# Moving gathered and scattered rows of a four-layer graph network from GpSimd to the SyncE and ScalarE queues, and splitting the K and V products over the halves of the array

## The chip, the core and the metric

The kernel runs on one core of a Trainium2 chip. The core has five engines with a queue of instructions each: TensorE (PE, its weight loads shown apart as PEld), VectorE (DVE), ScalarE (ACT), GpSimd (POOL) and SyncE (SP), which only issues transfers. All transfers run on the same 16 DMA engines. The metric is the time of one execution on the device in microseconds (us).

## What is computed

A graph with 12,500 nodes of 64 features and 400,000 edges, sorted by their target `dst`, goes through four layers, each followed by a residual sum and a layer norm. Cut to what matters:

```python
# layer 0: a message for every edge, the maximum over the edges of each target
h = relu(concat([x[dst], x[src] - x[dst]]) @ W1 + b1); out = segment_max(h @ W2 + b2, dst)
# layer 1: the mean of the edge attributes over the edges of each source
v_e = segment_sum(edge_attr, src) / max(count(src), 1)
out = relu(relu(concat([x, v_e, u]) @ W1 + b1) @ W2 + b2)
# layer 2: the mean of x[src] over the edges of each target, times a count of gates, a product
h = segment_sum(x[src], dst) / max(deg, 1); ...; out = (h * gates) @ W_lin.T + b_lin
# layer 3: attention with a weight matrix for each node type (4) and edge type (8), 4 heads
k, q, v = typed_linear(x, W, node_type)
a = (rel_att(k[src]) * rel_att(q[dst])).sum(-1) * rel_pri / sqrt(16)
out = typed_linear(segment_sum(softmax_over_dst(a) * rel_msg(v[src]), dst), Wa, node_type)
```

All is in float32 to the outside; `src` is random, so every x[src] is a gather of single rows.

## The kernel before, in words

Edges lie on 128 partitions ("lanes") of 3,125 consecutive edges each. A column of 128 edges, one for each lane, is called a tile; 25 columns are a group (`G`), 125 groups in all, in the edge loops 124 and three short ones. A running result goes along each lane: `keep` is 1 where an edge has the same target as the one before, so that `previous * keep + new` adds up a segment (line 1127 in layer 2, 1278 for q in layer 3). Results of all edges are written to memory (R0 to R3), and the row of each node's last edge is gathered from there.

Every gather of 128 rows is an indirect DMA on GpSimd, issued by the helper `gather` (line 211). The stages in the order of time:

- **Early part** (to about 1,270 us): 40 groups of x[src] are gathered for later use, counts are made by one-hot products on PE.
- **Scatter** (to about 5,380 us): the edge attributes, sorted anew by `src`, are scattered into the table SRT. `advance` (DVE, PE and ACT, in an order fixed by the program) works out the places of a group's edges in rounds of four tiles, `hot` loads the attributes into the buffer `at` (four buffers; lines 632 and 634: DVE writes the number of the source beside them), and `scatter` (line 734) sends 25 tiles of a group by indirect DMAs. It runs two groups behind `advance`. SP also writes zeros into the table S here.
- **Layer 0, with the sums of layer 1** (to about 8,140 us): gathers `gb` from TB; at the end the ends of lanes are put right (`ends_of_lanes`, `put_ends`).
- **Node stage of layers 0 and 1** (`nodes01`, to about 8,415 us): for each of 98 node tiles a gather from R0 (`ga`) and one from R1 (`g1`), blocks of 7.
- **Layer 2** (to about 12,280 us): gathers `gx` from X2, four buffers of a group; ACT's queue writes the sums to R2 (line 1130). In every third group, 3 to 123, the last tile is not gathered by GpSimd: SP loads 16 row numbers into registers (line 1112) and issues 16 DMAs of one row each (line 1117), eight times over. A row's address is worked out from its number by an instruction of its own.
- **Node stage of layers 2 and 3** (`nodes2`, to about 12,600 us): blocks of 7 node tiles in stages that interleave; a gather from R2, the gates, the layer norm, the products for q, k and v by node type (line 1221 writes K and V of a block into `kv`, K in partitions 0 to 63, V in 64 to 127), a put of the q rows into S by GpSimd (line 308), and for each tile two products of `kv` with `wkm` (line 1244), which ACT copies (line 1246) to `km` and SP writes to the table TKM: for each node and edge type 64 numbers of K and 64 of V. `wkm` has 128 rows; in each of its columns one half of them is zero.
- **Layer 3** (to about 16,550 us): gathers `gk` from TKM (3 buffers), loads of S into `st` (2 buffers, line 1273), then scores, running maximum, sums and messages, written to R3 by SP (line 1324).
- **Last node stage**: gathers from R3, the output product and the last layer norm.

A queue runs in order: an instruction that waits holds all that stand behind it in the same queue. Where the kernel says `manual_schedule(engines=...)`, these engines take the order in which the program is written; elsewhere a scheduler chooses it when the kernel is built.

Of the kernel before, what the change touches and what calls it, by code (L numbers as in the profile page):

```python
# [43 lines left out]
ACTN = 3  # L44
ROWS2 = 3
RL = 16
ZC = 200
# [3 lines left out]
def resnorm_gnn_kernel(ctx: ExitStack, tc: tile.TileContext, a: dict, out: bass.AP):  # L51
# [158 lines left out]
    def gather(to, table, at):  # L210
        return nc.gpsimd.indirect_dma_start(  # L211
            out=to, out_offset=None, in_=table, in_offset=bass.IndirectOffsetOnAxis(ap=at, axis=0)
        )

    def same_keys(psp, sb, key, n, each=None, want_count=False):
# [188 lines left out]

    wkm = const.tile([P, ETY, 2, D], F32, name="wkm")
    nc.vector.memset(wkm, 0.0)
    for h in range(NH):
        nc.sync.dma_start(
            wkm[D + h * HS : D + (h + 1) * HS, :, 1, h * HS : (h + 1) * HS],
            a["L3_gnn_rel_msg"][h].rearrange("t d o -> d t o"),  # L410
        )
# [226 lines left out]
    def turned(k):  # L638
# [6 lines left out]
        for j in range(m):  # L645
            nc.tensor.matmul(pT[:, j, :], oh[:, j, :], identh, start=True, stop=True)  # L646
        pH = ups.tile([NT, 2, P], F32, name="pH")
        for s, n in ((0, min(2, m)), (1, m)):
# [57 lines left out]
    now = [begin]  # L706
    todo = [0]

    def advance():

        k = todo[0]
        hot(k + 2)
        turned(k + 1)
        ol = work[k]["hots"][1]
        pG = spots(k)
        if k + 2 in work:
            work[k + 2]["tables"] = tables(now[0])
        pairs(k + 1)
        sums_of(k, pG, ol)
        todo[0] += 1  # L720

# [8 lines left out]
    def scatter(i, between=()):  # L730
        at, _, to = placed.pop(i)
        for j in range(G):

# [7 lines left out]
            if j % 4 == 0 and between:  # L741
# [3 lines left out]
                puts0.append(row)  # L745
        return put

# [73 lines left out]
    with tc.tile_pool(name="ini", bufs=1) as ini, tc.tile_pool(name="inips", bufs=1, space=PSUM) as ips:  # L821
# [31 lines left out]
        for t in range(ETY):  # L853
            pr_ = ips.tile([P, 4, P], F32, name="ps_k")[:D, 0, :D]
            nc.tensor.transpose(pr_, ratt[:, t, :], ident[:D, :D])
            rT = ini.tile([D, D], F32, name="rT", bufs=2)
            nc.vector.tensor_copy(rT, pr_)
            pg = ips.tile([P, 4, P], F32, name="ps_k")[:D, 0, :D]
            nc.tensor.matmul(pg, rT, rT, start=True, stop=True)
            nc.vector.tensor_scalar(wkm[:D, t, 0, :], pg, prib[:, t : t + 1], None, op0=ALU.mult)  # L860

# [59 lines left out]

    to_l0.close()

    with (tc.tile_pool(name="e0", bufs=2) as sb, tc.tile_pool(name="e0ps", bufs=2, space=PSUM) as psp,
# [81 lines left out]
        for g, (c0, ng) in enumerate(groups):  # L1006
# [25 lines left out]
            while done < NG and done * R1G <= g * NG:  # L1032
                key, pm1 = sums(done, key, pm1)
                done += 1
                if done == NG:
                    end_sums()
        row = ends_of_lanes(sb, R0, D)
        ps = carry_over(ps1, sb, pm)
        u = sb.tile([D, P], F32, name="u0", bufs=1)
        nc.vector.tensor_tensor_scan(u, neg64, ps, NEG, ALU.add, ALU.max)  # L1040
        nc.vector.tensor_max(row, row, shifted(ps1, sb, u, "g0"))
        put_ends(R0, row)


    with tc.tile_pool(name="n1", bufs=1) as sb, tc.tile_pool(name="n1ps", bufs=2, space=PSUM) as psp:
# [5 lines left out]
        def nodes01(b, t0, nt):  # L1051
# [6 lines left out]
            for j in range(nt):  # L1058
                gather(ga[:, j, :], R0[: E + 1, :], lastE[:, t0 + j : t0 + j + 1])
            g1 = tile_of([P, nt, D + 1], "g1")  # L1060
            for j in range(nt):
                gather(g1[:, j, :], R1[: E + 1, :], lastE1[:, t0 + j : t0 + j + 1])
            comb = tile_of([P, nt, 2 * D], "comb", 8)
# [27 lines left out]

        in_turn(nodes01, [NB] * (NBA - 1) + [4, 2, 1], lambda n: EVERY1)


    with tc.tile_pool(name="e2", bufs=2) as sb, tc.tile_pool(name="e2ps", bufs=1, space=PSUM) as psp:
        pm = sb.tile([P, D], F32, name="m2", bufs=1)
        nc.vector.memset(pm, 0.0)

        single = [g for g in range(2, NG - 1) if g % ROWS2 == 0]
        ns = len(single)  # L1100
        assert single == list(range(single[0], NG - 1, ROWS2)) and ns <= P
        at = groups[single[0]][0] + G - 1
        sf = sb.tile([P, ns], F32, name="sf", bufs=1)
        nc.vector.tensor_copy(sf, srcS[:, at : at + (ns - 1) * ROWS2 * G + 1 : ROWS2 * G])
        ps = psp.tile([P, P], F32, name="ps_i")
        nc.tensor.transpose(ps[:ns, :], sf, ident)
        numbers = sb.tile([P, P], I32, name="numbers", bufs=1)
        nc.vector.tensor_copy(numbers[:ns, :], ps[:ns, :])

        def row_by_row(to, k):  # L1110
            for p in range(0, P, RL):
                _, rows = nc.values_load_multi_w_load_instructions(
                    numbers[k : k + 1, p : p + RL], engines=[mybir.EngineType.SP], min_val=0, max_val=NP - 1,
                    skip_runtime_bounds_check_because="src is the number of a node",
                )
                for r, row in enumerate(rows):
                    nc.sync.dma_start(to[p + r : p + r + 1, :], X2[ds(row, 1), :])

        for g, (c0, ng) in enumerate(groups):
            gx = sb.tile([P, ng, D], F32, name="gx", bufs=4)  # L1120
            if g in single:
                row_by_row(gx[:, ng - 1, :], single.index(g))
            for j in range(ng - (g in single)):
                gather(gx[:, j, :], X2, srcS[:, c0 + j : c0 + j + 1])
            for j in range(ng):
                c = c0 + j
                nc.vector.scalar_tensor_tensor(gx[:, j, :], pm, keep[:, c : c + 1], gx[:, j, :],  # L1127
                                               op0=ALU.mult, op1=ALU.add)
                pm = gx[:, j, :]
            nc.scalar.dma_start(lanes(R2)[:, c0 : c0 + ng, :], gx)  # L1130
        row = ends_of_lanes(sb, R2, D)
# [33 lines left out]
    with tc.tile_pool(name="n2", bufs=1) as sb, tc.tile_pool(name="n2ps", bufs=2, space=PSUM) as psp:  # L1165
        puts = []

        def nodes2(b, t0, nt):
# [65 lines left out]
            for j in range(nt):  # L1234
# [5 lines left out]
                s = slice(j * P, (j + 1) * P)  # L1240
                km = sb.tile([P, 2, ETY * D], F32, name=f"km_{j % 4}")
                for w in range(2):
                    pw = psp.tile([P, ETY * D], F32, name="pw", bufs=4)
                    nc.tensor.matmul(pw, kv[:, s], wkm[:, w * ETY // 2 : (w + 1) * ETY // 2].rearrange("p e s f -> p (e s f)"),  # L1244
                                     start=True, stop=True)
                    nc.scalar.activation(km[:, w, :], pw, AF.Copy)
                r = (t0 + j) * P
                nc.sync.dma_start(
                    TKM[r * ETY : (r + P) * ETY, :].rearrange("(p e) f -> p (e f)", e=ETY),
                    km.rearrange("p w f -> p (w f)"),  # L1250
                )
# [6 lines left out]
    with tc.tile_pool(name="e3", bufs=2) as sb, tc.tile_pool(name="e3ps", bufs=1, space=PSUM) as psp:  # L1258
# [8 lines left out]
        last = G  # L1267
        for c0, ng in groups:
            gk = sb.tile([P, ng, 2 * D], F32, name="gk", bufs=3)
            for j in range(ng):  # L1270
                gather(gk[:, j, :], TKM, stS[:, c0 + j : c0 + j + 1])
            st = sb.tile([P, ng, D], F32, name="st", bufs=2)
            load = nc.sync.dma_start(st, lanes(S)[:, c0 : c0 + ng, :])
            for put in puts:
                after(load, put, "reads what they write")
            for j in range(ng):
                c = c0 + j
# [46 lines left out]
            nc.sync.dma_start(lanes(R3)[:, c0 : c0 + ng, :], R)  # L1324
            last = ng

        row = ends_of_lanes(sb, R3, W3)
# [113 lines left out]
```

## Time and profile before

| what | value |
|---|---|
| median of 3 runs | 16696.17 us (16695.95 to 16697.46) |
| profiled execution, as timed | 16699.22 us |
| span of its profile | 16697.4 us |
| indirect DMAs on GpSimd: scatter, layer 3, layer 2, layer 0 | 3125, 3125, 3084, 2125 |
| single-row DMAs on SP in layer 2 | 5248 (41 tiles) |
| mean rate of all transfers | 98 GB/s, 1640.30 MB |

A row of the costliest groups has the line, the engine, the operation, what it writes and reads, the count, then the busy time in us and the mean of one in ns, then the idle time of that engine just before these instructions with what ended most of it. "issue" means that the engine waited for nothing that the profile shows. A row of the waits has who waited, for whom, the time in all, how often, and the longest. Instructions of SP and of the other engines' sequencers (marked q) are not counted as busy.

### The profile page before, as it was taken

The numbers are of one execution on the slowest core, as the hardware profiler recorded it, in microseconds if no ns is written. First come the engines' busy times: TensorE is split into PE (matmuls) and PEld (weight loads), VectorE is DVE, ScalarE is ACT, GpSimd is POOL, SyncE is SP. The second block draws the span as 40 slices with busy tenths as digits, with TensorE's granted clock in tenths as the row PEclk, the third lists the DMA queues.
The fourth block names the chain that finished last, engine by engine and source line by source line (L and its number), as shares of the span: only waits on it lengthen the run. The fifth ranks groups of instructions, "written<-read, shape, count | busy, mean of one in ns | idle before, by whom it ended". The sixth has DMA issues, their size and how long they took to land. (4 is left out here: it accounts for less than half of the span.)

```text
span 16697.4 us, 162726 instructions
## 1 busy us (share of the span) xinstructions
PE 5362.8 (32%) x42392; PEld 4426.1 (27%) x42392; DVE 9601.6 (58%) x28242; ACT 2673.4 (16%) x4960; POOL 12548.5 (75%) x13066
## 2 busy tenths in 40 slices
PE   4445666666653666666400000000051000000002
PEld 4444555554542555555300000000030000000002
DVE  9996777777753777776322222222235565555556
ACT  0012333333321111111100000000022122122112
POOL 7777777777777777777777777777776777777776
PEclk6667777777766777777655555555575555555555
DMA  2333333222222555555211111111143333333333
GB/s 81 119 103 90 85 85 85 63 54 54 53 53 57 203 199 198 205 200 172 60 52 52 55 53 55 53 55 53 54 146 128 107 109 109 107 108 107 109 107 97
DMA packets 1116080, 1640.30 MB, mean 98 GB/s; under 512 B 740851, under 2 KB 741235, under 8 KB 1114755
## 3 DMA queue, kind: packets, MB, share of 16 engines
q1 hardware_dynamic: 653490, 987.85, 17.6%
q0 software_dynamic: 417824, 533.15, 12.2%
q10 hardware_dynamic: 43824, 108.83, 1.7%
q8 instruction: 337, 5.52, 0.1%
q14 instruction: 605, 4.95, 0.1%
HBM read 891.71 MB, written 737.15 MB: 98 GB/s over the span
## 5 line engine op out<-in xcount | busy, mean ns | idle before, releaser
L734 POOL DMA_INDIRECT SRT<-at,to x3125 | 3036.9, 972 | 952.5 <-issue 945.5
L211 POOL DMA_INDIRECT gk<-TKM,stS x3125 | 2975.6, 952 | 952.4 <-issue 926.8
L211 POOL DMA_INDIRECT gx<-X,srcS x3084 | 2921.0, 947 | 966.9 <-issue 907.5
L1127 DVE SCALAR_TENSOR_TENSOR gx<-gx,keep 128x64 f32<-128x64 f32 x3124 | 917.9, 294 | 2945.4 <-DMA gx<-X,srcS 1839.7
L211 POOL DMA_INDIRECT gb<-TB,srcS x2125 | 2076.0, 977 | 651.7 <-issue 625.2
L1028 DVE SCALAR_TENSOR_TENSOR R<-R,negm,msg 128x64 f32<-128x64 f32 x3124 | 854.0, 273 | 791.3 <-PE msg L959 786.9
L899 PE MATMUL ps_c<-ident,full 128*64 128x128 f32 x3 | 1.3, 421 | 3943.1 <-DVE full L1330 3942.0
L899 PE MATMUL ps_c<-ident,gx 128*64 128x128 f32 x1 | 0.4, 422 | 3867.6 <-DVE gx L1127 3867.6
L1285 DVE TENSOR_TENSOR pr<-st,gk 128x320 f32<-128x320 f32 x627 | 308.3, 492 | 1556.5 <-DMA gk<-TKM,stS 1551.5
L211 POOL DMA_INDIRECT xg<-in_x,srcS x1000 | 954.9, 955 | 306.0 <-issue 299.6
L899 PEld LDWEIGHTS ps_c<-ident,full 128*64 128x64 f32 x3 | 0.4, 129 | 3944.5 <-DVE full L1330 3942.8
L899 PEld LDWEIGHTS ps_c<-ident,gx 128*64 128x64 f32 x1 | 0.1, 129 | 3867.9 <-DVE gx L1127 3867.9
L337 DVE TENSOR_TENSOR ol<-iota,lo 128x512 f16<-128x512 f32 (+2 forms) x1000 | 979.1, 979 | 0.0
L1278 DVE SCALAR_TENSOR_TENSOR st<-st,keep 128x64 f32<-128x64 f32 x3124 | 868.4, 278 | 46.1
L953 PE MATMUL pt<-ident,st 128*128 128x128 f32 (+1 forms) x3250 | 825.9, 354 | 213.8 <-DVE st L1019 196.2
L1019 DVE SCALAR_TENSOR_TENSOR st<-st,keep 128x64 f32<-128x64 f32 x3124 | 863.7, 276 | 1.5
L694 PE MATMUL pG<-ol,mb 128*128 128x128 f16 x4625 | 778.0, 242 | 195.4 <-ACT mb L678 193.9
L987 DVE SCALAR_TENSOR_TENSOR r<-r,keep 128x64 f32<-128x64 f32 x3000 | 830.4, 277 | 0.1
L334 DVE TENSOR_TENSOR oh<-iota,hi 128x392 f16<-128x392 f32 (+2 forms) x1000 | 784.3, 784 | 24.0 <-DMA xg<-in_x,srcS 24.0
L646 PE MATMUL pT<-identh,oh 128*98 128x128 f16 x3125 | 413.3, 263 | 1180.3 <-DVE oh L334 1178.2
L952 PE MATMUL pt<-ident,gb 128*128 128x128 f32 (+1 forms) x2210 | 571.6, 353 | 565.6 <-DMA gb<-TB,srcS 561.3
L694 PE MATMUL pG<-A,hT 98*128 98x128 f16 x3125 | 732.3, 244 | 0.0
(325 smaller groups left out, 18349.9 us busy)
## 6 DMA issues: line engine op xcount, KB each, us to landing
st<-S SPq DMA_DIRECT2D x248, 800.0 KB
R<-R SPq DMA_DIRECT2D x124, 900.0 KB
r<-SRT SPq DMA_DIRECT2D x125, 812.5 KB
R<-r SPq DMA_DIRECT2D x125, 812.5 KB
S<-zero SPq DMA_DIRECT2D x200, 500.0 KB
R<-R SPq DMA_DIRECT2D x124, 800.0 KB
R<-gx ACTq DMA_DIRECT2D x124, 800.0 KB
gx<-X SPq DMA_DIRECT2D x5248, 0.2 KB
```

Of the source, the lines that this page charges most:

```text
L211: return nc.gpsimd.indirect_dma_start(out=to, out_offset=None, in_=table, in_offset=bass.IndirectOffsetOnAxis(ap=at, axis=0))
L334: nc.vector.tensor_tensor(oh, iota[:, None, :NT].to_broadcast([P, n, NT]), hi[:, :, None].to_broadcast([P, n, NT]), ALU.is_equal)
L337: nc.vector.tensor_tensor(ol, iota[:, None, :].to_broadcast([P, n, P]), lo[:, :, None].to_broadcast([P, n, P]), ALU.is_equal)
L694: nc.tensor.matmul(pG[:, j, :], l, r, start=(n == 0), stop=(n == len(terms) - 1))
L734: put = nc.gpsimd.indirect_dma_start(out=SRT, out_offset=bass.IndirectOffsetOnAxis(ap=to[:, j : j + 1], axis=0), in_=at[:, j, :], in_offse ...
L952: nc.tensor.matmul(pt[:w, k, :], two_tiles(gb, k, w), ident, start=True, stop=False)
L953: nc.tensor.matmul(pt[:w, k, :], two_tiles(st, k, w), ident, start=False, stop=True)
L987: nc.vector.scalar_tensor_tensor(r1[:, j, :D], pm1, keep1[:, c : c + 1], r1[:, j, :D], op0=ALU.mult, op1=ALU.add)
L1019: nc.vector.scalar_tensor_tensor(st[:, j, :], pa, keep[:, c : c + 1], st[:, j, :], op0=ALU.mult, op1=ALU.add)
L1028: nc.vector.scalar_tensor_tensor(R[:, j, :], pm, negm[:, c : c + 1], msg[:, j - q, :], op0=ALU.add, op1=ALU.max)
L1127: nc.vector.scalar_tensor_tensor(gx[:, j, :], pm, keep[:, c : c + 1], gx[:, j, :], op0=ALU.mult, op1=ALU.add)
L1278: nc.vector.scalar_tensor_tensor(st[:, j, :], pa, keep[:, c : c + 1], st[:, j, :], op0=ALU.mult, op1=ALU.add)
```

## The change

Tiles are taken off GpSimd's list and fetched or put row by row on other queues, in four places; two things go with it.

- **Layer 2**: 98 tiles in place of 41, the last two of groups g with g mod 5 equal to 1 or 3, one on SP and one on ACT. The rows of a group are issued two groups ahead; `gx` has 5 buffers; R2 is written by SP. SP and ACT take the program's order.
- **Layer 3**: the last tile of every third group on SP (41 tiles), in two halves of 64 rows, issued after the groups three and two before; `st` is loaded two groups ahead, behind R3, in 3 buffers. SP takes the program's order.
- **Scatter**: the last tile of every third group from 3 to 105 on SP (35 tiles). Its places are turned into a row by a transpose on PE and scaled on DVE, inside `advance`.
- The rows of layers 2 and 3 are addressed in bytes, from places that DVE has multiplied beforehand (`places_of`, `bytes_of`); one load of registers serves 32 rows (`RL`).
- **K and V**: `wkm` has 64 rows for K and 64 for V in the same columns; for each node tile one product uses partitions 0 to 63, the other 64 to 127, and the copies put them side by side.
- **Ends of R1**: the gathers for the first 28 node tiles are issued in layer 0's stage (`sums_early`), into `g1s`.

```diff
-ROWS2 = 3
-RL = 16
+ROWS2 = 5, (1, 3)
+ROWS3 = 3
+RL = 32
+ROWS1 = 3
...
+    def places_of(psp, sb, columns, size, name):
+        n = columns.shape[1]
+        f = sb.tile([P, n], F32, name=f"{name}_f", bufs=1)
+        nc.vector.tensor_copy(f, columns)
+        ps = psp.tile([P, P], F32, name="ps_i", bufs=1)
+        nc.tensor.transpose(ps[:n, :], f, ident)
+        t = sb.tile([n, P], I32, name=name, bufs=1)
+        nc.vector.tensor_scalar(t, ps[:n, :], float(size), None, op0=ALU.mult)
+        return t
+    def row_by_row(table, size, p, *parts):
+        rows = [
+            nc.values_load_multi_w_load_instructions(
+                places[:, p : p + RL], engines=[kind], min_val=0, max_val=table.shape[0] - size,
...
+            )[1]
+            for engine, kind, to, places in parts
+        ]
+        for r in range(RL):
+            for (engine, kind, to, places), at in zip(parts, rows):
+                engine.dma_start(to[p + r : p + r + 1, :].bitcast(mybir.dt.uint8), table[None, ds(at[r], size)])
...
     def scatter(i, between=()):
         at, _, to = placed.pop(i)
-        for j in range(G):
+        for j in range(G - (i in single1)):
...
+        for p in range(0, P, RL):
+            _, spots_ = nc.values_load_multi_w_load_instructions(
+                in_a_row[i][:, p : p + RL], engines=[mybir.EngineType.SP], min_val=0, max_val=E - 1,
...
+            for r, spot in enumerate(spots_):
+                put = nc.sync.dma_start(SRT[ds(spot, 1), :], at[p + r : p + r + 1, G - 1, :])
...
+        sums_early(NS - 8)
         row = ends_of_lanes(sb, R0, D)
+        sums_early(5)
...
+        single = [g for g in range(2, NG - 1) if g % ROWS2[0] in ROWS2[1]]
...
+        with tc.manual_schedule(engines={SP, ACT}):
+            for g, (c0, ng) in enumerate(groups):
+                if g + 2 in single:
+                    to, k = tiles_of(g + 2), 2 * single.index(g + 2)
+                    for p in range(0, P, RL):
+                        row_by_row(X2b, 4 * D, p, (nc.sync, SP, to[:, G - 2, :], places[k : k + 1, :]),
+                                   (nc.scalar, ACT, to[:, G - 1, :], places[k + 1 : k + 2, :]))
+                gx = tiles_of(g)
+                for j in range(ng - 2 * (g in single)):
+                    gather(gx[:, j, :], X2, srcS[:, c0 + j : c0 + j + 1])
...
+                nc.sync.dma_start(lanes(R2)[:, c0 : c0 + ng, :], gx)
...
-                for w in range(2):
-                    pw = psp.tile([P, ETY * D], F32, name="pw", bufs=4)
-                    nc.tensor.matmul(pw, kv[:, s], wkm[:, w * ETY // 2 : (w + 1) * ETY // 2].rearrange("p e s f -> p (e s f)"),
+                pws = [psp.tile([P, ETY, D], F32, name="pw", bufs=4) for _ in range(2)]
+                for w, pw in enumerate(pws):
+                    of = slice(w * D, (w + 1) * D)
+                    nc.tensor.matmul(pw.rearrange("p e f -> p (e f)"), kv[of, s], wkm[of].rearrange("p e f -> p (e f)"),
                                      start=True, stop=True)
-                    nc.scalar.activation(km[:, w, :], pw, AF.Copy)
+                for w, pw in enumerate(pws):
+                    nc.scalar.activation(km[:, :, w, :], pw, AF.Copy)
...
+            if g + 2 < len(groups):
+                load_starts(g + 2)
+            for ahead, half in ((3, 0), (2, 1)):
+                if g + ahead in single:
+                    to, k = keys_of(g + ahead)[:, G - 1, :], single.index(g + ahead)
+                    for p in range(half * P // 2, (half + 1) * P // 2, RL):
+                        row_by_row(TKMb, 8 * D, p, (nc.sync, SP, to, places3[k : k + 1, :]))
```

## The prediction

> **What bounds the kernel now.** I read the first line of the page (busy time by engine), then its costliest groups, then what GpSimd (POOL) waited for, then the busy time of every engine by stage.
>
> ```profile
> PE 5362.8 (32%) x42392; PEld 4426.1 (27%) x42392; DVE 9601.6 (58%) x28242; ACT 2673.4 (16%) x4960; POOL 12548.5 (75%) x13066
> ...
> L734 POOL DMA_INDIRECT SRT<-at,to x3125 | 3036.9, 972 | 952.5 <-issue 945.5
> L211 POOL DMA_INDIRECT gk<-TKM,stS x3125 | 2975.6, 952 | 952.4 <-issue 926.8
> L211 POOL DMA_INDIRECT gx<-X,srcS x3084 | 2921.0, 947 | 966.9 <-issue 907.5
> ```
>
> The reader should add the two times of each row: busy plus idle before, over the count. A scatter tile costs POOL (3036.9 + 952.5) / 3125 = 1.277 us, a layer-3 tile 1.257 us, a layer-2 tile (966.9 less one start wait of 26.7) 1.252 us. The idle part is "issue", 0.30 us each time: nothing else holds POOL. 13,057 such DMAs at about 1.26 us are 16.45 of the 16.70 ms, so POOL is the bound although it shows only 75% busy. True waits of POOL are few:
>
> ```profile
> POOL S L308 <- ACT q L1231: 51.6, 5, 11.8
> POOL row L211 <- DMA R<-R: 28.3, 2, 16.3
> POOL gx L211 <- DMA X<-xs: 26.7, 1, 26.7
> ```
>
> By stage (scatter; layer 2; layer 3; and the node stage between them, cut at POOL's last gather), columns PE, PEld, DVE, ACT, POOL busy, granted clock, DMA share, GB/s:
>
> ```profile
> 1400.00:5300.00 3900.00, 2360.63 (x24117) 1900.29 (x24115) 2871.04 (x6752) 1164.88 (x2506) 2968.79 (x3056) 0.75 0.25 66
> 8430.00:12270.00 3840.00, 0.00 (x0) 0.00 (x0) 908.11 (x3090) 0.00 (x0) 2904.74 (x3068) 0.50 0.19 53
> 12660.00:16520.00 3860.00, 0.00 (x0) 0.00 (x0) 2285.38 (x6513) 777.51 (x861) 2924.21 (x3071) 0.50 0.33 108
> 12291.00:12499.00 208.00, 196.44 (x780) 115.38 (x781) 91.16 (x224) 109.96 (x214) 157.90 (x161) 0.95 0.65 221
> 12499.00:12601.00 102.00, 97.67 (x389) 56.31 (x386) 34.11 (x84) 56.68 (x105) 34.92 (x36) 1.00 0.58 212
> ```
>
> In the first three POOL issues back to back and DVE is at 74%, 24% and 59%. In the node stage the first 208 us are POOL's (161 DMAs, 1.29 us each) and in the last 102 us PE is 96% busy at full clock while POOL has 36 DMAs: there PE is the bound.
>
> **The gathers taken off POOL.** Layer 2 had 41 single tiles (groups 3, 6, ... 123) and gets 98 (two of each of 49 groups), so 57 leave POOL; layer 3 loses 41, the scatter 35. 57 x 1.252 = 71.4, 41 x 1.257 = 51.5, 35 x 1.277 = 44.7: together 167.6 us. POOL's program has exactly 133 indirect DMAs less. This is worth its full value only if the rows arrive before POOL, or the ring of buffers, needs them.
>
> **What a row costs its queue.** Layer 2 has them already:
>
> ```profile
> L1117 SPq FUSED_REGOPS  x5248: 37/37/52, 8417.2 to 12273.2; - x195
> L1117 SPq MOVE gx<-X x5248: 29/29/38, 8417.8 to 12273.3; - x195
> L1117 SPq DMA_DIRECT2D gx<-X x5248: 224/225/955, 8417.9 to 12273.3; - x195
> ...
> L1112 SPq TENSOR_LOAD <-numbers x328: 1134/1252/1662, 8415.9 to 12265.7; - x164
> ...
> 8999.97 5.97 SPq L1117 DMA_DIRECT2D gx<-X  x15
> ```
>
> Fifteen rows in 5.97 us, the last one's 0.225 off: 0.41 us from row to row. The three instructions make 0.291, so each has a gap of 0.04. With byte offsets made once by DVE (the place times 256 or 512) the FUSED_REGOPS falls away: 0.41 - 0.037 - 0.04 = 0.33 us. The scatter keeps it: 0.41. One load of registers now serves 32 rows instead of 16; bounds 1.25 to 2.5 us (the length of one or of two old loads), I take 1.25. Against the time POOL needs:
>
> - Layer 2, five groups: POOL 121 x 1.252 = 151.5 us. SyncE 256 x 0.33 + 8 x 1.25 + 5 writes of R2 at 0.33 = 96; ScalarE 94. Both queues issue at once, which no row shows. If their DMA instructions excluded each other wholly, a row would take 2 x 0.225 = 0.45 us: 127. It fits either way; the edge is (151.5 - 11.7) / 256 = 0.546 us a row.
> - Layer 3, three groups: POOL 74 x 1.257 = 93; SyncE 128 x 0.33 + 4 x 1.25 + 3 x 0.64 (R3 and st) = 49. The rows stand behind R3, which waits for the group's end, hence two halves of 64; a half is 24 us in a period of 31, and lands a group ahead of its reader. The st loads move behind R3 too, with a third buffer, one group early.
> - Scatter, three groups: POOL 74 x 1.277 = 94.5; SyncE 128 x 0.41 + 4 x 1.25 + about 3 x 3 for the at and S loads = 67.
>
> **What is queued behind.** In the scatter the at load of a fourth group now waits behind the rows, and DVE waits for that buffer before it goes on:
>
> ```profile
> SPq L634 <- DMA SRT<-at,to: 3318.1, 348, 43.5
> SPq L1117 <- DMA R<-gx: 1204.2, 102, 32.9
> ...
> DVE at L632 <- DMA SRT<-at,to: 766.8, 102, 78.0
> ```
>
> SyncE idles 3318 us in the scatter stage, so it has the room. DVE idles 766.8 us over some 122 groups, 19 us in three; its work in a cycle of 94.5 is thus 76 us. Rows start when POOL ends the group before and are out 67 + 2 us later, 36 later than POOL's own puts of that group. DVE then works 76 us and is back at 145, which is 50 us into the next cycle where the buffer comes at 69: three short waits become one of 19 us and POOL, two groups behind DVE, never sees it. Slack 19 / 128 = 0.15 us a row. The 35 small transposes and scalings lie in the same idle time. In layer 2, R2's writes move from ScalarE to SyncE behind 48 us of rows: R2 of that group is some 17 us late, with five buffers where POOL needs its slot two groups later. So: nothing for all of this; bounds 0 and the whole gain of the scatter and half of layer 2, 80 us.
>
> A rule against single rows stands in the Trainium skill, DMA: Bandwidth & Descriptors, section Rules for kernel authors: coalesce many small transfers, since a small one pays mostly overhead, about 2.0 us each by that page. Paid one after the other that would be 256 us a tile and lose milliseconds; the row of 0.41 us shows that they overlap, and the trace decides.
>
> **Moved gathers.** 28 gathers of R1's ends move from the node stage of layers 0/1 to the end of layer 0. In POOL's order all stand before the last 100 gb gathers, so they fill nothing of the 16.3 us wait for R0: 28 x 1.2 = 34 us later there, 34 sooner afterwards. Bounds -16 (that wait filled after all) and +34 (the next stage can't use it); I take 0, as its PE is busy only 140 of 350 us.
>
> **K and V in halves.** Each tile had two products with 128 rows of contraction, of which K needs 64 and V the other 64; now one uses rows 0 to 63, the other 64 to 127, 512 columns as before.
>
> ```profile
> 12441.66 10.57 PE L1244 MATMUL pw<-wkm,kv 128*128 128x512 f32 x24
> ...
> L1246 ACT ACTIVATE km<-pw x196: 575/597/599, 12312.1 to 12596.7; 128x512 f32<-128x512 f32 x196
> ```
>
> 0.44 us an instruction, four a tile, 1.76. No trace here shows two halves at once: bounds are no overlap (gain 0) and full overlap (0.88 a tile). A block of seven takes 102 / 5 = 20.4 us of PE now; with overlap 14.2, or 16.4 if ScalarE's copies (14 x 0.6 = 8.4) pace the products. Five blocks of tail: 20 to 31 us; the lag that PE gathers behind POOL in the first part (about 2.3 us a block, nine blocks) goes too: 20 to 50 in all. I take 35.
>
> The Trainium skill, TensorEngine Tiling (Array Packing), section Key Properties, says that different tiles of the array can run their loads and matmuls in parallel, and section PSUM Bottleneck that emptying PSUM may then be the limit. By the first the gain is as taken; no run here shows it yet.
>
> **Sum.** 167.6 + 35 = 203 off the profiled execution's span of 16697.4 (16699.2 as timed): 16496. The median of the runs, 16696.2, lies 3 below that time, so I say 16495.
>
> **Rivals.**
> - The halves bring nothing (they run one after the other, or ScalarE's copies hold PE): 16696 - 168 = 16528. For it: no row of this trace shows overlap. Against: PE is plainly the bound of those 102 us and works on half-empty rows.
> - One stage gives its gain back: rows late in the scatter (45 us), or POOL's gathers 2 to 3% longer beside two row queues (3027 x 0.03 = 90): 16545 to 16620. For it: gathers of the scatter take 972 against 944 ns, so their length can vary. Against: in layer 2 they take 940/944/1014 (min, median, max) with and without rows beside them.
> - Slower: SyncE and ScalarE become the bound of layer 2. Their rows share one count of landings, so a slow queue holds the other. From 0.546 us a row POOL waits, at 25 x (256c - 139.9) = 203, c = 0.58, the whole gain is gone, at 0.6 the time is 16495 + 343 = 16840. For it: a row has taken up to 0.955. Against: the median is 0.225, and even mutual exclusion gives 0.45.
> - The change doesn't take POOL's work away: its order says otherwise; about 16696.
>
> **Chances.** Forecast 0.50 (16465 to 16515), halves idle 0.27, one stage lost 0.11, slower 0.09, no change 0.03. Range 16460 (28 gathers filling the wait, full overlap) to 16600. Within 0.2% (33 us, about what a measurement of this kernel can tell from no change) 0.03; faster 0.88; slower 0.09.
>
> **What would show it.** POOL's per-DMA times stay at 1.25 to 1.28; counts 3027, 3084 and 3090; rows at 0.33 (layer 2 and 3) and 0.41 us; DVE's wait at the at column in fewer, longer pieces; the node stage's tail from 102 to some 67 us. Wrong if POOL shows waits on DVE or on gx, gk rows, or PE's pw still takes 0.88 us a product.

## The result, and the profile after

The changed kernel takes 16498.47 us (median of 4, 16497.10 to 16502.24), the kernel before beside it 16696.06: a ratio of 0.9882, 95% interval 0.9865 to 0.9899. The forecast was 16495 us. Cut by the times at which GpSimd's (POOL's) DMAs begin and end, the two profiled executions (spans 16697.4 and 16495.3 us) compare so:

| stage | before | after | difference | forecast |
|---|---|---|---|---|
| to the end of the scatter | 5384.4 | 5340.2 | -44.2 | -44.7 |
| layer 0 | 2749.4 | 2780.0 | +30.6 | +34 |
| node stage 0/1 | 283.3 | 247.0 | -36.3 | -34 |
| layer 2 | 3868.7 | 3787.6 | -81.1 | -71.4 |
| node stage 2/3 | 316.4 | 289.4 | -27.0 | -35 |
| layer 3 | 3939.7 | 3895.3 | -44.4 | -51.5 |
| rest | 155.6 | 155.8 | +0.2 | 0 |

The sum is right to 1 us, but by misses that cancel, which is luck: layer 2 brings 10 more than forecast and the two rows of the moved gathers 6 more, node stage 2/3 and layer 3 bring 15 less. First the page of the changed kernel, busy time by engine and costliest groups (columns as before):

```profile
PE 5308.2 (32%) x42428; PEld 4391.4 (27%) x42428; DVE 9765.8 (59%) x28328; ACT 2661.4 (16%) x4960; POOL 12402.4 (75%) x12933
...
L778 POOL DMA_INDIRECT SRT<-at,to x3090 | 3004.1, 972 | 942.3 <-issue 908.1
L213 POOL DMA_INDIRECT gk<-TKM,stS x3084 | 2927.7, 949 | 940.3 <-issue 924.5
L213 POOL DMA_INDIRECT gx<-X,srcS x3027 | 2860.2, 945 | 951.1 <-issue 893.5
```

Busy plus idle over the count again: 1.277 us in the scatter as before, 1.254 in layer 3 (1.257 before), 1.250 in layer 2 (1.252; in both the one wait for X, 27.6 us now, is taken off). The counts are down by 35, 41 and 57, and the idle part is still nearly all "issue": no queue of rows holds POOL on the way. Then POOL's waits:

```profile
POOL row L213 <- DMA R<-R: 44.8, 2, 27.6
POOL gx L213 <- DMA X<-xs: 27.6, 1, 27.6
POOL S L341 <- ACT q L1306: 25.1, 4, 9.7
```

The wait for ScalarE's q is halved (51.6 before), which belongs to node stage 2/3. But the wait for R at the ends of layers 0 and 3 has grown from 28.3 to 44.8 us, and its longest piece, 27.6, is now the end of layer 3 (12.0 before). Busy time by stage (columns as before: PE, PEld, DVE, ACT, POOL, granted clock, DMA share, GB/s) for the scatter, layers 2 and 3, and node stage 2/3 up to and after POOL's last gather in it:

```profile
1400.00:5300.00 3900.00, 2355.86 (x24165) 1890.67 (x24165) 2880.52 (x6792) 1168.55 (x2509) 2968.72 (x3055) 0.76 0.25 67
8400.00:12100.00 3700.00, 0.00 (x0) 0.00 (x0) 866.79 (x3033) 0.00 (x0) 2796.65 (x2961) 0.50 0.21 55
12500.00:16300.00 3800.00, 0.00 (x0) 0.00 (x0) 2445.53 (x6465) 769.47 (x854) 2876.12 (x3031) 0.50 0.36 109
12160.00:12368.00 208.00, 178.51 (x858) 109.39 (x859) 99.78 (x243) 112.62 (x235) 157.94 (x161) 0.95 0.71 240
12368.00:12443.00 75.00, 62.42 (x310) 38.76 (x308) 26.00 (x66) 41.76 (x84) 35.61 (x36) 0.98 0.65 238
```

The last two rows are the reading of the halves: the tail is 75 us where it was 102, and PE is busy 83% of it, no longer 96%. PE has 310 instructions left in the tail where it had 389, and 858 in the first part where it had 780: at POOL's last gather PE is now a block further.

### The profile page after: what moved, and what is told of

The parts are those of the page before. It is cut to its first block, busy times and chain, and to the rows that moved or that the text cites. A ratio compares the mean times of both kernels' runs of the same rounds, so it can differ in the third digit from the quotient of the medians.

```text
span 16495.3 us, 195146 instructions
## 1 busy us (share of the span) xinstructions
PE 5308.2 (32%) x42428; PEld 4391.4 (27%) x42428; DVE 9765.8 (59%) x28328; ACT 2661.4 (16%) x4960; POOL 12402.4 (75%) x12933
## 5 line engine op out<-in xcount | busy, mean ns | idle before, releaser
L213 POOL DMA_INDIRECT gk<-TKM,stS x3084 | 2927.7, 949 | 940.3 <-issue 924.5
L213 POOL DMA_INDIRECT gx<-X,srcS x3027 | 2860.2, 945 | 951.1 <-issue 893.5
```

Of the source, the lines that this page charges most:

```text
L213: return nc.gpsimd.indirect_dma_start(out=to, out_offset=None, in_=table, in_offset=bass.IndirectOffsetOnAxis(ap=at, axis=0))
```

## Experiments

Twelve runs. "Before" is the kernel before, run beside it on the same chip.

| run | time | before | ratio, 95% interval |
|---|---|---|---|
| full_width | 16525.58 | 16698.17 | 0.9896 (0.9880 to 0.9913) |
| no_scatter_rows | 16542.41 | 16698.17 | 0.9906 (0.9889 to 0.9922) |
| no_l3_rows | 16553.24 | 16698.17 | 0.9913 (0.9897 to 0.9930) |
| l2_122 | 16837.54 | 16698.17 | 1.0083 (1.0066 to 1.0099) |
| gk4 | 25621.29 | 24558.90 | 1.0429 (1.0412 to 1.0446) |
| dve_copy | 26265.34 | 24558.90 | 1.0694 (1.0676 to 1.0712) |
| g1_late | 26232.58 | 24558.90 | 1.0679 (1.0661 to 1.0696) |
| l2_sp_only | 26226.16 | 24558.90 | 1.0676 (1.0655 to 1.0698) |
| four_edits | 16536.76 | 16726.76 | 0.9886 (0.9869 to 0.9902) |
| three_edits | 16486.79 | 16697.08 | 0.9874 (0.9858 to 0.9891) |
| pool_in_order | 26175.03 | 24552.02 | 1.0660 (1.0646 to 1.0675) |
| pool_in_order_2 | 16491.62 | 16728.76 | 0.9857 (0.9841 to 0.9874) |

The runs beside which the kernel before took some 24,555 us were on chips numbered 0 (gk4, dve_copy, g1_late, l2_sp_only) and 13 (pool_in_order); they are told of by themselves below, and these times are not compared with the others. Beside four_edits and pool_in_order_2 the kernel before took 16,727 to 16,729 us, 0.18% more than beside the rest, and gathers followed each other 0.2 to 0.4% more slowly in these two runs; why is open, and the chip's number does not tell it, since three_edits was on chip 3 like pool_in_order_2, beside 16,697 us.

**The halves of the array (full_width).** The old products again:

```diff
...
-                    nc.tensor.matmul(pw.rearrange("p e f -> p (e f)"), kv[of, s], wkm[of].rearrange("p e f -> p (e f)"),
+                    nc.tensor.matmul(pw, kv[:, s], wkm[:, w * ETY // 2 : (w + 1) * ETY // 2].rearrange("p e s f -> p (e s f)"),
...
```

> The changed kernel with the old K and V products (128 rows of contraction, half of them zero; the copies as they were). Theory: the two half-array products overlap, and what they save is the tail of node stage 2/3: it goes back from 75 to about 102 us after POOL's last gather, the time to 16498 + 27 = 16525, and pw shows 0.44 us an instruction. Rival: the 27 us of that stage come from what else changed there, the halves bring nothing: 16498 and a tail of about 75 us.

Measured: 16525.58, 27.1 more than the changed kernel, and from POOL's last gather to the first of layer 3 104.4 in place of 77.4 us (counted from the start of the gather): the theory to the microsecond. PE's timeline (start, length, engine, line, operation, count, wait), first two blocks with full width, then two of the changed kernel, then the start of the first of these by itself:

```profile
12418.54 10.57 PE L1319 MATMUL pw<-wkm,kv 128*128 128x512 f32 x24
...
12439.17 10.57 PE L1319 MATMUL pw<-wkm,kv 128*128 128x512 f32 x24
```

```profile
12299.06 4.40 PE L1320 MATMUL pw<-wkm,kv 64*128 64x512 f32 x15
12304.29 2.77 PE L1320 MATMUL pw<-wkm,kv 64*128 64x512 f32 x8 [0.83 <-ACT km L1323]
...
12317.70 4.40 PE L1320 MATMUL pw<-wkm,kv 64*128 64x512 f32 x15
```

```profile
12299.06 1.93 PE L1320 MATMUL pw<-wkm,kv 64*128 64x512 f32 x7
```

An instruction lasts 0.59 us in both kernels, and the next begins before it ends. From one start to the next are (10.57 - 0.59) / 23 = 0.43 us with full width; with halves they are (1.93 - 0.59) / 6 = 0.22 in the first seven, and (4.40 - 0.59) / 14 = 0.27 in all fifteen, before PE waits for a copy. So the halves do run beside each other, fully as long as a buffer for the product is free, and then ScalarE's copies set the pace. This agrees with the Trainium skill, TensorEngine Tiling (Array Packing), sections Key Properties (tiles can run in parallel) and PSUM Bottleneck (emptying PSUM may then limit). The block as a whole goes from 20.6 us (12439.17 - 12418.54) to 18.6 (12317.70 - 12299.06). ScalarE is not full: it is busy 112.62 of the 208 us of the first part. Its copies of a block stand between its other steps; more than four buffers for the products were not tried.

**The rows of the scatter (no_scatter_rows).**

```diff
-    single1 = range(ROWS1, HISTG - ROWS1, ROWS1)
+    single1 = range(0)
```

> The changed kernel with all tiles of the scatter on POOL again, rows of layers 2 and 3 kept. Theory: 35 puts at 1.277 us come back whole, 16498 + 45 = 16543, POOL's time per put stays 1.277, and DVE's wait at the at column goes back from 607 to about 767 us in some 100 pieces. Rival: a part of the 44 us seen in that stage is paid elsewhere (35 transposes and scalings, later starts of what follows): about 16520.

Measured: 16542.41, 43.9 more; the scatter ends at 5384.2 again. The 35 puts are worth their full price. What DVE waits for before it writes the `at` column in the changed kernel (us, times):

```profile
  DMA SRT<-at,to: 607.0, 58
  DMA SRT<-at: 153.5, 17
```

760.5 us in 75 pieces where it was 766.8 in 102, and is 769.8 in 103 again without the rows: about the same idle time in fewer and longer pieces, and POOL does not see it.

**How near the row queues are to their edge (l2_122).** 122 single tiles in layer 2:

```diff
-ROWS2 = 5, (1, 3)
+ROWS2 = 2, (1,)
```

> The changed kernel with two single tiles in every second group of layer 2: 122 tiles in place of 98. Theory: SyncE and ScalarE are far from being the bound; for two groups SyncE needs 128 x 0.33 + 4 x 2.2 + 2 x 0.33 = 52 us and POOL 48 x 1.25 = 60, so 24 more gathers go for nothing: 16498 - 30 = 16468. Rival: the two queues are nearer to their edge than their own times say (contention of rows, R2 late behind them): POOL waits on gx, and the time stays at 16498 or goes above it.

Measured: 339 us more, although POOL has 24 gathers less. The rival is right, and it is the slow case of the prediction. What waits in layer 2 of this run (us, times, longest), then SyncE's timeline:

```profile
DVE gx L1201 <- DMA gx<-X: 2687.2, 56, 55.6
...
POOL gx L213 <- DVE gx L1201: 308.0, 48, 12.0
```

```profile
9999.93 46.71 SPq L244 DMA_DIRECT2D gx<-X  x97
10046.90 0.84 SPq L1204 DMA_DIRECT2D R<-gx  x2
10052.79 16.78 SPq L244 DMA_DIRECT2D gx<-X  x36
```

Between the second and the third line SyncE loads registers, 4.9 us long, beside R2's transfers; its other gaps are waits, told of below. From one batch of 128 rows to the next are 66 us, where POOL needs 48 x 1.25 = 60. So a row costs 66 / 128 = 0.516 us all in, not the 96 / 256 = 0.375 (loads and writes of R2 included) that I took. In the changed kernel five groups thus ask 2 x 66 = 132 us of SyncE against POOL's 151.5: the margin was 19, not 55 us. Two terms were too small. The first are the loads, in the changed kernel:

```profile
L236 SPq TENSOR_LOAD <-places x360: 2064/2220/4731, 8400.7 to 16280.6; - x180
L236 ACTq TENSOR_LOAD <-places x196: 1965/2298/2467, 8369.7 to 12038.7; - x196
```

A load of 32 registers takes 2.2 us (min, median, max in ns), near my upper bound, and up to 4.7 beside large transfers. The second is the row itself: with two queues at work 128 rows take some 60 us, where SyncE alone in layer 3 issues 64 in 23.4 (below), 47 for 128. What SyncE waits for in layer 2 of l2_122 (us, times, longest):

```profile
SPq L244 <- DMA gx<-X: 559.0, 1877, 3.8
```

That is 9 us in each of the 61 batches, and it is a wait for rows to land. In the trace every row of SyncE waits for one of eight semaphores, which the program gives to the transfers of both queues in turn: it waits until the earlier transfer with the same semaphore has landed. With two queues that is the row four before on the same queue (6486 of SyncE's 7808 rows), with SyncE alone in layer 3 the row eight before (4592 of 5248). The landing that a held row waited for came 1.76 us (median) after its issue: later than four steps of 0.34 us, sooner than eight, and in layer 3 of this run no wait for a row is found. So most of the 13 us between 47 and 60 are this wait: the second queue slows the first by taking half of the semaphores. Whether more semaphores would remove it was not tried. In the changed kernel the same wait is 577.5 us in 1021 pieces. That the second queue slows the first was to be tested by itself:

> One single tile in every second group of layer 2, on SyncE alone, none on ScalarE (61 tiles). For the cost of a row: in the changed kernel both queues issue at once and 128 rows take 60 us on each. Theory: the two queues slow each other, alone SyncE needs 128 x 0.33 + 3 loads x 2 = 48 us, as in layer 3. Rival: 60 us is what SyncE needs beside POOL's gathers in any case. The time is 16498 + 37 x 1.25 = 16544 by both.

```diff
-ROWS2 = 5, (1, 3)
+ROWS2 = 2, (1,)
...
-                        row_by_row(X2b, 4 * D, p, (nc.sync, SP, to[:, G - 2, :], places[k : k + 1, :]),
-                                   (nc.scalar, ACT, to[:, G - 1, :], places[k + 1 : k + 2, :]))
+                        row_by_row(X2b, 4 * D, p, (nc.sync, SP, to[:, G - 1, :], places[k + 1 : k + 2, :]))
...
-                for j in range(ng - 2 * (g in single)):
+                for j in range(ng - (g in single)):
...
```

It ran on chip 0, told of below, where 128 rows took a median of 99 us on SyncE alone and of 134 with both queues (the run g1_late). SyncE's wait for rows in layer 2, first alone, then with both:

```profile
SPq L244 <- DMA gx<-X: 44.9, 83, 1.4
```

```profile
SPq L244 <- DMA gx<-X: 388.1, 452, 5.3
```

The direction is the theory's and the wait nearly goes, as the semaphores would have it; the size can't be carried over.

**The end of layer 3.** Six runs and two wrong theories. First the rows of layer 3 away:

```diff
-        single = list(range(3, NG - 1, ROWS3))
+        single = []
```

> The changed kernel without single rows in layer 3; the st loads stay behind R3, two groups ahead, in three buffers. Theory: in layer 3 a loop of R3, rows and DVE keeps R3 some 46 us behind POOL's last gather of a group and costs 15.5 us at the end; without rows the 41 gathers come back (51.5) and the 15.5 go: 16498 + 36 = 16534, last R3 about 11 us behind the last gather. Rival: the st loads behind R3 make the lag: 16498 + 51 = 16549 with R3 as late as now.

Measured: 16553.24, 54.8 more than the changed kernel. The wait at the end does fall, from 28.5 to 12.4 us (here and below from the start of the last gather; POOL's own wait is 0.9 less), but layer 3 as a whole is 54.1 us longer: 41 gathers are back, and all are longer:

```profile
L213 POOL DMA_INDIRECT gk<-TKM,stS x3125 | 2985.9, 955 | 952.4 <-issue 942.6
```

1.260 us a gather against 1.254: 19 us over 3125. So 41 gathers (51.5), less 16 at the end, plus 19. Why the gathers are longer without the rows is not settled. Next, what I held to be a loop, opened with a fourth buffer:

```diff
-            gks[g] = sb.tile([P, groups[g][1], 2 * D], F32, name="gk", bufs=3)
+            gks[g] = sb.tile([P, groups[g][1], 2 * D], F32, name="gk", bufs=4)
...
-            for ahead, half in ((3, 0), (2, 1)):
+            for ahead, half in ((3, 0),) * (g == 0) + ((4, 0), (3, 1)):
```

> The changed kernel with a fourth buffer for gk and the two halves of a row tile issued one group earlier (after the groups four and three before). Theory: the rows now land a group before DVE needs them, the loop R3, rows, DVE opens, R3 falls back from 46 to about 16 us behind POOL's last gather and the wait at layer 3's end from 27.6 to about 12: 16498 - 15 = 16483. Rival, from the run without rows, whose gathers were 19 us longer in all: with R3 and the st load so early in the period the gathers beside them grow by some 10 to 20 us, and the time stays within 16493 to 16503.

On chip 0 layer 3 took 5330 us where three other kernels took some 5900; that says nothing of the loop. The same edit ran again with three others, each in a stage of its own:

> The changed kernel with one edit in each of four stages, so that each is read from its own stage: (1) layer 0: 12 of the 28 gathers of R1's ends behind the last gather of edges; (2) layer 2: two single tiles in four of nine groups, 108 in place of 98; (3) node stage 2/3: the copies of V on DVE; (4) layer 3: a fourth gk buffer, rows a group earlier. Theory: (1) 12 x 1.22 = 14.6 us fill the 17 us wait for R0: layer 0 from 2780 to 2765 us; (2) 54 pairs of tiles at 66 us are 3564 us for the two row queues, under POOL's 3017 x 1.25 = 3771: layer 2 from 3788 to 3775; (3) ScalarE's copies no longer pace the products: the tail from 77 to 60 to 72 us; (4) the loop of R3, rows and DVE opens, the last wait falls from 28.5 to 12 to 16 us: layer 3 from 3895 to about 3882. Sum 16498 - 50 = 16448. Rivals: (1) the row of lane ends is later by as much, 2780; (2) the queues are the bound where two such groups stand two apart, and layer 2 is over 3788; (3) the copies delay DVE's own steps, tail 77 or more; (4) gathers grow beside R3 and st, by up to 19 us in all: 3895 or more.

The wait at layer 3's end stayed at 27.3 us although the rows were out some 20 us before the last gather of the group ahead of theirs, and 13 after it in the changed kernel: no loop. The other three edits are told below. Then the order of DVE, in a run that has the edits of layers 0 and 2 too:

```diff
-        with tc.manual_schedule(engines={SP}):
+        with tc.manual_schedule(engines={SP, ACT, mybir.EngineType.DVE}):
```

> The changed kernel with (1) 12 gathers of R1's ends behind the last gather of edges and (2) 108 single tiles in layer 2, both as in the run with four edits, three gk buffers and the copies on ScalarE as in the changed kernel, and (3) in layer 3 DVE and ScalarE in the order in which the program is written, as SyncE already is. In the changed kernel DVE's order there was chosen when the kernel was built: it has the 25 steps of q of the next group ahead of a group's scores, where the kernel without rows has them between. Theory: this order, not the landing of the rows, keeps R3 46 us behind POOL's last gather; in the order of the program R3 is some 16 us behind it, the wait at the end of layer 3 falls from 28.5 to 12 to 14 us, and with (1) and (2) the time is 16498 - 15 - 8 - 15 = 16460. Rival: rows that stand behind R3 keep it late whatever DVE's order is: the wait stays at 28 us and the time at 16475. Second rival: R3 is early again, but gathers grow beside R3 and the st load as in the kernel without rows, by up to 19 us in all: 16475 to 16480 with a short wait at the end.

Measured: the wait grew to 34.5 us and layer 3 to 3909.9. No again. But DVE's timeline now showed groups whose 25 tiles were all there at once, between groups that waited for each tile. The order of POOL's instructions in the built kernels explains it (left the changed kernel, its first six buffers with their gathers; right, POOL in the order of the program):

```
gk_143254 x25   group 0        gk_147129 x25   group 0
gk_143357 x24   group 3        gk_147427 x25   group 1
gk_143552 x25   group 1        gk_147724 x25   group 2
gk_143849 x25   group 2        gk_147232 x24   group 3
gk_144053 x24   group 6        gk_148123 x25   group 4
```

A buffer of 24 gathers is a group with a single tile. Its buffer is asked for three groups early, for the rows, and when the kernel is built all its gathers move up with it. DVE must take the groups in order, so after the last gather of 122 a whole group, 123, is left to do, with the short groups behind it. My "46 us late" was a count of gathers by 25 that gave them to the wrong groups.

So POOL was put in order, again beside the edits of layers 0 and 2:

```diff
-        with tc.manual_schedule(engines={SP}):
+        with tc.manual_schedule(engines={SP, mybir.EngineType.Pool}):
```

> The changed kernel with edits (1) and (2) of the run before (layer 0 to 2767.5, layer 2 to 3777.5 us, together -22.5) and (3) in layer 3 POOL in the order in which the program is written, beside SyncE; DVE and ScalarE as the build chooses. What the order of the built kernels shows: because the buffer of a single-row group g + 3 is asked for in step g, POOL gathers groups in the order 0, 3, 1, 2, 6, 4, 5, ... 123, 121, 122; so the R3 that I read as 46 us late belongs to groups whose gathers stand 30 us later (16 + 30), and at the end a whole group's work of DVE and ScalarE (group 123, which has to follow 122) is left after the last gathers. Theory: with POOL in order the wait at the end falls from 28.5 to 12 to 14 us, R3 follows each group's last gather by 16, layer 3 goes from 3895 to about 3880 and the time to 16498 - 22 - 15 = 16461. Rival: the order costs nothing, the rows' landing behind R3 is what delays the end: the wait stays near 28 us, 16475. Second rival: the end is shorter, but R3 and st fall on other gathers and lengthen them by 9 to 19 us as in the kernel without rows: 16470 to 16480.

It fell on chip 13, with 24,552 us for the kernel before, where the end can't be read, and was run again:

> The same kernel as in the run with POOL in order, again, since the kernel before took 24,552 us there and POOL waited for transfers in every stage, so that the end of layer 3 could not be read. Theory, on a chip where the kernel before takes about 16,697: the wait at the end of layer 3 is 12 to 14 in place of 28.5 us, layer 3 takes about 3880, the time is 16461. Rival: the wait stays near 28, 16475. Second rival: a short wait, but gathers longer by 9 to 19 us in all: 16470 to 16480.

Measured: the wait at the end is 13.4 us, R3 follows each group's last gather by 15 to 17 us all along, and POOL's wait for R at the ends of layers 0 and 3 is, for both together,

```profile
POOL row L213 <- DMA R<-R: 15.0, 2, 12.5
```

against 44.8 (27.6 the longest). SyncE's timeline in layer 3, the changed kernel first:

```profile
13439.11 0.32 SPq L1415 DMA_DIRECT2D R<-R  x1
...
13444.75 23.41 SPq L244 DMA_DIRECT2D gk<-TKM  x64
13480.81 0.36 SPq L1415 DMA_DIRECT2D R<-R  x1
...
13486.16 23.72 SPq L244 DMA_DIRECT2D gk<-TKM  x64
13512.11 0.36 SPq L1415 DMA_DIRECT2D R<-R  x1
...
13532.27 0.32 SPq L1415 DMA_DIRECT2D R<-R  x1
```

```profile
13453.66 0.36 SPq L1420 DMA_DIRECT2D R<-R  x1
...
13484.25 0.36 SPq L1420 DMA_DIRECT2D R<-R  x1
...
13514.35 0.32 SPq L1420 DMA_DIRECT2D R<-R  x1
```

R3 (the lines R<-R) goes out 42, 31 and 20 us apart in the changed kernel, and 31, 30 apart with POOL in order. Counted in the built order, R3 of the changed kernel follows the last gather of its group by 15 us in two groups of three and by 98 in those with a single tile, whose gathers were done two groups early. The theory of the end stands. What it is worth is less sure: layer 3 takes 3891.7 us, not 3880, only 3.6 less than in the changed kernel, since a gather takes 1.258 in place of 1.254 us, some 12 us in all. In this run a put of the scatter, too, costs 1.280 in place of 1.277 us, which as a share would make 8 of the 12; the rest may be the second rival, longer gathers beside an earlier R3, and is not told apart.

**Copies on DVE (dve_copy, and the third of the four edits).**

```diff
-                    nc.scalar.activation(km[:, :, w, :], pw, AF.Copy)
+                    (nc.vector.tensor_copy(km[:, :, 1, :], pw) if w else nc.scalar.activation(km[:, :, 0, :], pw, AF.Copy))
```

> The changed kernel with the copies of V (one of the two for each node tile) on DVE in place of ScalarE. Theory: after the overlap ScalarE's copies pace the products; PE's wait for ACT km falls from 60 us to under 20, the stage's tail from 77 to some 60 to 72 us, the time to 16480 to 16493. Rival: the stage is held by its chain of small steps (PE and DVE in turn), the copies come into DVE's way, and the time is 16498 or up to 15 more.

Worse in both runs: node stage 2/3 took 418.9 us beside some 392 of the other kernels on chip 0, and 314.4 (tail 101.4) in four_edits, against 289.4 (77.4). Nearly the whole gain of the halves is gone. The tile km in four_edits, what its copies waited for and who waited for them (us, times):

```profile
L1328 DVE COPY km<-pw x98: 628/691/693, 12187.0 to 12467.4; 128x512 f32<-128x512 f32 x98
...
  PE pw L1325: 75.2, 61
  issue: 62.4, 10
...
  PEld pw L1325: 65.5, 71
  PE pw L1325: 27.4, 13
```

A copy on DVE takes 0.69 us, not 0.60, and it stands in DVE's fixed order between the layer norms of other blocks: DVE idles until the product is there, PE waits for the copy.

**Filling the wait for R0 (g1_late, and the first edit of three runs).** In g1_late 20 gathers were held behind the edges (`t >= NS - 20`), in the later runs 12:

```diff
...
+                if NS - 20 <= t < NS - 8:
+                    tc.add_manual_dep(
+                        g1.ins, last_gb.ins.name,
+                        mybir.DependencyInfo(mybir.DependencyClass.NoSync, mybir.DependencyReason.DATA), reason="behind the edges",
+                    )
...
```

> The changed kernel with the last 20 of the 28 gathers of R1's ends held behind the last gather of edges in layer 0. Theory: 12 to 14 of them then fill POOL's 17 us wait for the last R0, which they now only precede: 16498 - 15 = 16483. Rival: the row of lane ends queues behind them, so that what fills the wait delays the chain of lane ends by as much: 16498 and above.

With 20 the row of lane ends went out 45.9 us after the last gather of edges, 23.0 in the other three kernels on chip 0: it queued behind them, the rival. With 12 the theory held: in three_edits layer 0 took 2767.5, 12.5 less than in the changed kernel. The same run's second edit, 108 single tiles in layer 2, took 3777.5, 10.1 less: there the queues' 54 x 66 = 3564 us still fit. With the longer gathers of four_edits and pool_in_order_2 the same two edits gave 2772.8 and 2772.2 us in layer 0, and 3788.1 and 3783.3 in layer 2: the gain of layer 2 was read in one run alone.

**Two slow chips.** gk4, dve_copy, g1_late and l2_sp_only ran on chip 0, the first pool_in_order on chip 13, where the kernel before took 24,552 to 24,559 us. POOL's gathers have the same length there (median 944 to 947 ns), but in some stretches of SyncE's queue each instruction, a register move of 0.029 us as well as a DMA, lasts 0.70 us, and PE has gaps too that no wait explains. SyncE's rows in l2_sp_only:

```profile
15010.54 98.97 SPq L244 DMA_DIRECT2D gx<-X  x128
```

A row is two or three instructions of a queue, and the five kernels, which have many more rows than the kernel before, are 4 to 7% slower there than it. That the rows make them slower is not shown: layer 0, which has none, takes 4248.4 us in g1_late in place of 2780.0, and layer 2 takes 6530.2 with 61 single tiles and 6527.5 with 98. The changed kernel itself was not run there, nor is there a trace of the kernel before. What holds the queues is open.

## Why the prediction came out right, step by step

- **133 gathers at POOL's price**: right. The prices of 1.25 to 1.28 hold, the scatter's term to half a microsecond, and taking the rows away gives it back. Layer 2 brought 81.1 in place of 71.4: 3027 gathers of 1.250 in place of 1.252 make 6, an end wait of 4.0 in place of 7.5 on R2 the rest.
- **What a row costs its queue**: the sign was right, the size wrong, and it did not show because there was room. "SyncE 256 x 0.33 + 8 x 1.25 + 5 writes of R2 at 0.33 = 96" is 132. The load of 32 registers costs 2.2, the upper half of its bounds, and both queues together stay just within the 0.45 that I gave as the worst, if the loads are taken out (60 less 3 x 2.2, over 127 steps: 0.42). But the reason is not the one I had: the instructions do not exclude each other, rows wait for earlier rows to land. The scatter's 0.41 us came as said. The Trainium skill (DMA: Bandwidth & Descriptors, section Anatomy of one DMA) puts the fixed part of a transfer from GpSimd at about 2.0 us, most of it the time until the landing is confirmed. In a queue this is not paid row after row (0.34 us alone, 0.52 with everything), but it shows where a row waits for an earlier landing, 1.76 us here.
- **The slow rival**: its mechanism is real, with 24 tiles more the row queues are the bound of layer 2. It was given 0.09 from an edge of 0.546 us a row without loads and writes, where the row cost 0.42. All in, the edge was 151.5 / 256 = 0.592 us and the row 0.516; in l2_122 the edge is 60 / 128 = 0.469.
- **Layer 3**, "lands a group ahead of its reader": the 64 rows of a half take 23.4 us, and 28 with the load ahead of them (24 said for both). What failed is that I took POOL's order for granted. The build put the gathers of every third group two groups early, which shows in no wait on the way and costs 15.5 us at the end: 36 of the 51.5 were left, and gathers 0.003 us shorter (3084 x 0.003 = 9), which nothing here explains, gave back part.
- **The scatter's DVE wait**: fewer, longer pieces as said, at no cost.
- **Moved gathers**: +30.6 and -36.3, a gain of 6 where I took 0, and what makes the 6 is open; that "they fill nothing of the 16.3 us wait" was right (17.3 now).
- **The halves**: overlap as taken, then held by ScalarE's copies as in the second case of the working, but worth less. A block takes 18.6 us, not the 16.4 of that case or the 14.2 of full overlap: the copies stand between ScalarE's other steps, and PE waits 60 us for them in the whole stage. The gain is 2.0 us in each of some 13 blocks, 27 us, not 35. About 2 us a block came in the first part, as said (2.3): after POOL's last gather PE has the products of four blocks left (112 instructions), where it had five (140). What came short is the gain of the blocks behind it, 2 us each in place of 4 to 6.

**A better version, perhaps.** pool_in_order_2 (POOL in order in layer 3, 12 gathers behind the edges, 108 single tiles) is 0.9857 of the kernel before, the changed kernel 0.9882. The intervals overlap, so that it is faster is not shown by the times. Its stages speak for it: against the changed kernel 7.8 us are off layer 0, 4.3 off layer 2 and 15 off the wait at the end of layer 3, with every gather a little longer; three_edits had 12.5 and 10.1 in the first two.

## What to carry to other kernels

Price a queue all in, loads of registers, waits for earlier landings and the other queue included, and find its edge by one run that goes beyond it: a change that is free at 132 of 151 us is a loss of 339 at the next step. Read what the queue itself waits for: two queues that share a set of semaphores have half of it each. When a buffer is asked for early, look at the built order of every engine that writes it; the order can change without any wait to show it. When a sum is right, check it by stage before believing its terms, and count the blocks that a stage has left before dividing its time by them.

## What the runs showed of the hardware

- Rows of 512 bytes on SyncE alone went out each 0.34 us (layer 3), rows of 256 on SyncE and ScalarE together each 0.42 to 0.43 on each queue (l2_122), where a row had to wait for the landing of the one four before; such a landing came 1.76 us after its issue (median).
- A load of 16 registers took 1.25, of 32 2.2 us, and up to 5 beside transfers of 800 KB.
- Two float32 products on 64 rows each of the array, 512 columns: an instruction began each 0.22 us with both halves at work, against 0.43 on 128 rows; each took 0.59 from start to end.
- On two chips (0 and 13) the kernel before took 47% longer; in the traces from there POOL's gathers had the same length.
